# The first and the last microseconds of a two-layer lookup convolution: norm ahead of the sort, transfers in another order, a last image of its own

## The chip, the core and the metric

The kernel runs on one core of one Trainium2 chip, in float32. The metric is the device time of one execution in microseconds, the median of several runs. Six sequences of instructions run side by side: TensorE (PE, with its weight loads PEld), VectorE (DVE), ScalarE (ACT), GpSimd (POOL) and SyncE (SP). Two of them issue transfers here: SP (queue q1 in the profile, "hardware_dynamic") and POOL (queue q0, "software_dynamic"). Both queues share 16 DMA engines.

## The reference

The input x has 16 images of 256 channels and 28 x 28 pixels. With g = the group norm of x (32 groups of 8 channels), the result is x + block(g), where block is two lookup convolutions with batch norms, a squeeze-and-excite gate, and a residual:

```python
def amm_conv3x3(x, centroids, w_sub):
    p = patches3x3(x)                            # (b, n, c, 9): 9 taps of every channel
    d = sum(p*p) - 2 * einsum('bncs,cks->bnck', p, centroids) + sum(centroids**2)
    attn = softmax(-d, axis=-1)                  # over 16 codes per channel
    lut = einsum('cks,cso->cko', centroids, w_sub)
    return einsum('bnck,cko->bno', attn, lut)

def block(g):
    out = relu(bn(amm_conv3x3(g, centroids1, wsub1)))
    out = bn(amm_conv3x3(out, centroids2, wsub2))
    s = sigmoid(relu(mean(out) @ w1 + b1) @ w2 + b2)
    return relu(out * s + g)

result = x + block(gn(x))
```

## The kernel before, in words

**Units.** Layer l of image b is cut into two halves of the pixels (384 and 400, `PXT`), and each half into 8 quads `m` of 32 channels. One quad of one half is a unit of 16 blocks: 16 small matmuls for the logits (`logits`, L591; 32 records in the profile), an exponential on ACT (`b_exp`, L643), 16 small matmuls with the codes (`b_num`, L653), two transposes and a reciprocal on DVE (`b_turn`, L665, L671), a scaling on POOL (`c_scale`, L681 to L693), a transpose on DVE (`c_turn`, L699), and dense matmuls with the weights (`c_look`, L717). After the 8 quads of a half, `evacuate` takes the sums from PSUM on ACT: into the image `ims[1]` for layer 1 (L729), into `y` with a running sum for layer 2 (L739). In layer 2, quad 0 is done with row maxima (`MAXED`), and its logits come five slots early.

**The plan.** `Plan` is a table from (slot, position) to calls; `emit` walks it in order, so it fixes each engine's program by hand. One slot holds one unit; a stage is one layer of one image, 16 slots. Stages run (layer 1 of image 0), (layer 1 of image 1), (layer 2 of image 0), (layer 1 of image 2), and so on, 32 stages or 512 slots. The last position of a slot, REST, holds the side work: loads, norms, shifts, patch writes.

**Patches.** The 9 taps are laid out in DRAM first. `shift` (ACT, L485 and L487) makes two copies of an image, moved by one column (`sides`); `to_pat` (L496) writes the image and the two copies to a DRAM buffer `pat`, 12 pieces in the order `STEPS` (half of the partitions h, column dx, block k); `patches` (L577, SP) reads a unit's rows from there with four transfers, three slots ahead. Units 0 to 3 of a half need the six pieces with h = 0. `prep` issues 12 pieces with all 784 pixels (588 KB), `prep_near` 24 pieces, the 384 pixels of the first half (288 KB) ahead of the 400 of the second (300 KB).

**Start.** SP and POOL load image 0 (`load_x`, POOL, L150) and the constants (SP). DVE and PE sort the channels: keys (`sort_keys`, L272 to L290), ranks (`sort_ranks`, L298 to L308), then the layer-1 weights by matmuls with the permutation (`sort_ws1(0)` to `sort_ws1(5)`, L333). `square_codes` (POOL, L419) and `setup_codes` (L426, L427) finish the codes. Group norm is `gn_stats` (DVE, L444), `gn_mean` and `gn_var` (PE, ACT, POOL), `gn_apply` (ACT, L475). Layer 2's weights are fetched by POOL with indirect transfers (`fetch_ws2`, L406, 18 of them), its codes are placed by SP (`place_wd2`, L365, `place_cw2`, L374).

**End of an image.** `se_hidden` and `se_gate` make the gate, `se_scale` (DVE, L536, L537) finishes it; then, in four blocks of 392 pixels, `gate` (ACT, L547), `finish` (DVE, L553, adds the normed image), `relu` (ACT, L557) with `residual` (POOL, L561) or `relu_residual` (DVE, L565), and one `store` (POOL, L568).

**Fallback.** POOL keeps running totals of the softmax sums. At the end DVE takes their extremes (`good`, L928, L929), PE and DVE count them into a flag (`bad`, L935), every engine loads the flag (L936), and behind it stands `tc.If(flag > 0)` with a loop that does all images again with maxima everywhere (L937). With these inputs the branch goes past it. The program's closing drains and barrier stand under L1031.

Of the kernel before, what the change touches and what calls it, by code (L numbers as in the profile page):

```python
# [72 lines left out]
def kernel(  # L73
# [74 lines left out]
    def load_x(b, xb):  # L148
        t = xpool.tile([P, NB, HW], F32, tag="xt", name="xt")
        nc.gpsimd.dma_start(t, xb.rearrange("(b p) n -> p b n", p=P))  # L150
        xs[b] = t

    load_x(0, x[0])


# [137 lines left out]
    def sort_ranks(row):  # L293
        own = small.tile([P, NB], F32, name="key_own")
        rank = small.tile([P, NB], F32, name="rank")
        for b in range(NB):
            dg = scratch(P)
            nc.vector.tensor_mul(dg, row[:, b * P : (b + 1) * P], ident)  # L298
            nc.vector.tensor_reduce(own[:, b : b + 1], dg, axis=AX.X, op=ALU.add)

            gt = scratch(C)
            eq = scratch(C)
            nc.vector.tensor_scalar(gt, row, own[:, b : b + 1], None, op0=ALU.is_gt)
            nc.vector.tensor_scalar(eq, row, own[:, b : b + 1], None, op0=ALU.is_equal)
            nc.vector.tensor_mul(eq, eq, earlier[:, b])
            nc.vector.tensor_add(gt, gt, eq)
            nc.vector.tensor_reduce(rank[:, b : b + 1], gt, axis=AX.X, op=ALU.add)
            nc.vector.tensor_scalar(perm[:, b], ranks, rank[:, b : b + 1], None, op0=ALU.is_equal)  # L308
# [258 lines left out]
    def store(b, ob):  # L567
        nc.gpsimd.dma_start(ob.rearrange("(b p) n -> p b n", p=P), ys.pop(b)[0])  # L568
        for d in (se, nrm, xs):
            d.pop(b)  # L570

# [178 lines left out]
    class Plan:  # L750
        def __init__(self, step, lead, lb):
            self.step = step
            self.lead = lead
            self.lb = lb
            self.ns = len(PXT) * NQ * step
            self.lc = LC if step == 1 else 3
            self.end = self.ns + self.lc * step
            self.jobs = {}
            self.tiles = []
            self.loads = []  # L760
# [56 lines left out]
        def prep(self, l, pat, t, pace=1):  # L817

            for i, dx in enumerate((0, 2)):
                for k in range(NB):  # L820
                    self.at(t + (2 * i + k if pace == 1 else i), REST, shift, l, dx, k)
            for i in range(len(STEPS)):
                self.at(t + int(i * pace), REST, to_pat, l, i, pat)

        def prep_near(self, l, pat, t):

            for i, dx in enumerate((0, 2)):
                for k in range(NB):
                    self.at(t + i, REST, shift, l, dx, k)
            n = len(STEPS) // 2  # L830
            for i, (dx, k, h) in enumerate(STEPS):
                self.at(t + i // 2, REST, to_pat, l, i, pat, *PXT[0])

                self.at(t + 6 if dx == 1 else t + 7 + 3 * h + (i - n * h - NB) * 3 // 4, REST, to_pat, l, i, pat, *PXT[1])

        def norm(self, b, t):
# [5 lines left out]
            for k in range(NB):  # L842
                self.at(t + k, REST, gn_apply, b, k)

        def close(self, b, ob, te, pace):
# [11 lines left out]
            self.at(te + 5 + 3 // pace, REST, store, b, ob)  # L857
# [11 lines left out]
    bn_setup()  # L869
    row = sort_keys()  # L870
    square_codes()
    for k in range(NB):
        for i in range(2):
            gn_stats(0, k, i)
    gn_mean(0)
    gn_var(0)
    sort_ranks(row)
# [3 lines left out]
    for i, (dx, k, h) in enumerate(STEPS[: len(STEPS) // 2]):  # L881
        if dx != 1:
            shift(0, dx, k)
        to_pat(0, i, d_pat[0], *PXT[0], eng=nc.gpsimd if dx == 0 else nc.sync)
    sort_bn()
# [3 lines left out]
    for si, (l, b) in enumerate(stages):  # L889
        t = si * NS  # L890
        plan.stage(l, b, pat_of(l, b), t, () if l == 0 else MAXED)
        if l == 0 and b >= 1:
            n0 = 7 if b == 1 else t - 2 * NS + 1
            plan.at(n0 - (8 if b == 1 else 11), REST, load_x, b, x[b])
            plan.norm(b, n0)
            plan.prep(0, pat_of(0, b), {1: 9, 2: 33, 3: 57}.get(b, t - 2 * NS + 3), 0.67 if b == 1 else 1)
        if l == 1:
            if b in (0, B - 1):
                plan.prep_near(1, pat_of(1, b), t - NS + LC)
# [3 lines left out]
            plan.close(b, out[b], t + NS + LC, 1 if b < B - 2 else 4)  # L903
    for i in range(len(STEPS) // 2, len(STEPS)):
        plan.at(-1, REST, to_pat, 0, i, d_pat[0], *PXT[0], nc.sync)
    for i in range(len(STEPS)):
        plan.at(i * 5 // len(STEPS), REST, to_pat, 0, i, d_pat[0], *PXT[1])
    for i, (slot, pos) in enumerate(((-1, REST), (-1, REST), (-1, REST), (0, LOOK_A), (1, LOOK_A), (1, LOOK_B))):
        plan.at(slot, pos, sort_ws1, i)
        if i % 2:  # L910
            plan.at(slot, REST, ones_row, pts[3 + i // 2])
# [4 lines left out]
    for g in range(NLT):  # L916
        plan.at(6 + g, REST, fetch_ws2, g)
# [6 lines left out]

    good = small.tile([P, 2], F32, name="good")
    for i, lim in enumerate((S_MAX, 1.0 / S_MIN)):
        t = small.tile([P, 1], F32, name="ext")
        nc.vector.tensor_reduce(t, totals[i], axis=AX.X, op=ALU.max)  # L928
        nc.vector.tensor_scalar(good[:, i : i + 1], t, lim, None, op0=ALU.is_le)  # L929
# [7 lines left out]
    with tc.If(flag > 0):  # L937
        with tc.For_i(0, B) as bi:
            load_x("g", x[bass.ds(bi, 1)].rearrange("o c n -> (o c) n"))
            plan = Plan(8, 3, 5)  # L940
# [7 lines left out]
            plan.at(s1 + plan.end - 4, REST, load_x, "g", x[bass.ds(bi, 1)].rearrange("o c n -> (o c) n"))  # L948
# [86 lines left out]
```

## Time and profile before

| | us |
|---|---|
| median of 3 runs | 2786.48 (2784.22 to 2790.07) |
| the profiled execution, its own time | 2784.22 |
| its span (first to last instruction) | 2782.7 |
| first logits matmul | 39.95 |
| last matmul of the lookups ends | 2759.7 |
| flag ready (L935) | 2769.81 |
| mean granted TensorE clock | 0.991 |

The page gives busy times over the whole span. Most of the span is one pattern of 32 slots, repeated, so the page's shares tell of that pattern; the two ends show only in answers to a window: the timeline, the chain of waits, busy time by stretch, and transfers by queue. A unit's beginning is read from the timeline's L591 rows, one group of 32 records per unit. Times in them count from the span's start.

### The profile page before, as it was taken

To read this page: it belongs to the slowest core of one execution; us is meant where nothing else is said; L and a number is where in the kernel's file an instruction comes from. 1 tells how busy PE (TensorE), PEld (TensorE's weight loads), DVE (VectorE), ACT (ScalarE), POOL (GpSimd) and SP (SyncE) were. 2 spreads that over 40 slices of the span, in tenths; PEclk is the share of its full clock that TensorE was granted. 3 is DMA by queue.
4 is the path that set the end of the run, shared out by engine and by line. 5 is a ranking of instruction groups with operands and counts; after the bars stand their busy time and mean duration, and the time that the engine had idled before them with its cause. 6 is when DMAs were issued, how large, how long until landed. Compare 5 with 4: busy or idle time off the path is not lost.

```text
span 2782.7 us, 90173 instructions
## 1 busy us (share of the span) xinstructions
PE 2706.4 (97%) x37748; PEld 1081.3 (39%) x37748; DVE 2180.1 (78%) x2645; ACT 1093.1 (39%) x1595; POOL 1902.7 (68%) x2714
## 2 busy tenths in 40 slices
PE   6999999999999999999999999999999999999996
PEld 3333333333333343333333333333333334333332
DVE  4667788887878878788887888778787787878885
ACT  2333443434334343443434334343443434334332
POOL 3786676766677677676766677667676766766763
PEclk9999999999999999999999999999999999999998
DMA  7887888767677676777767678676777767674551
GB/s 215 214 215 190 224 218 211 200 174 199 171 206 208 165 200 162 206 196 182 201 174 199 176 201 212 159 199 165 207 197 182 199 172 203 176 191 114 143 139 37
DMA packets 230825, 514.99 MB, mean 185 GB/s; under 512 B 34184, under 2 KB 185608, under 8 KB 230408
## 3 DMA queue, kind: packets, MB, share of 16 engines
q0 software_dynamic: 51824, 269.50, 36.7%
q1 hardware_dynamic: 178584, 239.62, 33.3%
q8 instruction: 299, 4.90, 0.7%
q14 instruction: 118, 0.97, 0.1%
HBM read 264.64 MB, written 244.37 MB: 183 GB/s over the span
## 4 chain that ended last, share of the span: by engine, by line
PE 85%; DVE 8%; issue 3%; POOL 2%; DMA 1%; ACT 0%; SPq 0%; DVEq 0%; POOLq 0%; ACTq 0%
PE acc L717 54%; PE pair L591 15%; PE pair L653 14%; DVE nt L665 3%; DVE q L699 1%; DVE rc L671 1%; DVE e L629 1%; POOL k L681 1%; DMA pat<-side 0%; POOL pat L496 0%; POOL total L693 0%; PE pair L333 0%; DMA pt<-pat 0%; PE pair L524 0%; DVE gn_st L444 0%
## 5 line engine op out<-in xcount | busy, mean ns | idle before, releaser
L717 PE MATMUL acc<-q,ws 128*128 128x384 f32 (+1 forms) x4096 | 1635.2, 518 | 4.5 <-ACT im L729 4.5
L665 DVE STREAM_TRANSPOSE nt<-pair 128x832 f32<-128x832 f32 (+1 forms) x1024 | 978.3, 993 | 528.2 <-PE pair L653 441.0
L681 POOL TENSOR_TENSOR k<-nt,rc 128x832 f32<-128x832 f32 (+1 forms) x512 | 803.8, 1570 | 825.8 <-DVE rc L671 786.9
L643 ACT ACTIVATE e<-pair 128x768 f32<-128x768 f32 (+1 forms) x960 | 740.2, 821 | 1045.2 <-PE pair L591 1044.5
L717 PEld LDWEIGHTS acc<-q,ws 128*128 128x128 f32 x4096 | 699.9, 189 | 889.6 <-issue 555.2
L591 PE MATMUL pair<-pt,wd 19*32 19x384 f32 (+1 forms) x16384 | 519.4, 501 | 27.4 <-DVE nt L665 17.2
L699 DVE STREAM_TRANSPOSE q<-k 128x832 f32<-128x832 f32 (+1 forms) x512 | 488.7, 954 | 0.8 <-POOL k L681 0.8
L653 PE MATMUL pair<-e,cw 32*32 32x384 f32 (+1 forms) x16384 | 484.6, 501 | 0.3 <-DVE nt L665 0.2
L671 DVE RECIPROCAL rc<-nt 128x104 f32<-128x104 f32 (+1 forms) x512 | 398.7, 779 | 17.6
L591 PEld LDWEIGHTS pair<-pt,wd 19*32 19x32 f32 x16384 | 125.5, 103 | 341.0 <-issue 241.7
L687 POOL TENSOR_TENSOR tail<-nt,rc 128x104 f32<-128x104 f32 (+1 forms) x512 | 243.1, 475 | 0.0
L653 PEld LDWEIGHTS pair<-e,cw 32*32 32x32 f32 x16384 | 119.8, 103 | 288.4 <-issue 169.9
L717 PE MATMUL acc<-qt,ws 128*128 128x400 f32 (+1 forms) x512 | 215.2, 502 | 0.0
L693 POOL TENSOR_TENSOR total<-total,nt 128x96 f32<-128x96 f32 (+1 forms) x480 | 213.3, 444 | 0.0
L693 POOL TENSOR_TENSOR total<-total,rc 128x96 f32<-128x96 f32 (+1 forms) x480 | 188.1, 392 | 0.0
L496 POOL DMA_DIRECT2D pat<-side x274 | 185.4, 677 | 3.4 <-ACT side L485 3.0
L636 ACT ACTIVATE e<-e 128x768 f32<-128x768 f32 (+1 forms) x64 | 54.9, 857 | 191.1 <-DVE e L629 190.0
L717 PEld LDWEIGHTS acc<-qt,ws 128*128 128x128 f32 x512 | 93.4, 190 | 88.6 <-issue 30.2
L729 ACT ACTIVATE im<-acc,bnsh,bnsc 128x384 f32<-128x384 f32 (+1 forms) x64 | 43.4, 679 | 149.6 <-PE acc L717 139.4
L621 POOL TENSOR_TENSOR z<-z,mx 128x768 f32<-128x768 f32 (+1 forms) x64 | 99.0, 1546 | 0.0
L496 POOL DMA_DIRECT2D pat<-im x136 | 92.4, 680 | 0.0
L739 ACT ACTIVATE y<-acc,bnsh,bnsc 128x384 f32<-128x384 f32 (+1 forms) x64 | 43.5, 679 | 89.4 <-PE acc L717 85.0
(121 smaller groups left out, 901.4 us busy)
## 6 DMA issues: line engine op xcount, KB each, us to landing
pat<-side POOLq DMA_DIRECT2D x232, 588.0 KB, 5.7
pt<-pat SPq DMA_DIRECT2D x1024, 112.5 KB
pt<-pat SPq DMA_DIRECT2D x1024, 108.0 KB
pat<-im POOLq DMA_DIRECT2D x116, 588.0 KB, 5.3
xt<-in_x POOLq DMA_DIRECT2D x32, 784.0 KB, 7.2
out_dram<-y POOLq DMA_DIRECT2D x16, 784.0 KB, 6.4
pat<-side POOLq DMA_DIRECT2D x24, 300.0 KB, 6.5
pat<-side POOLq DMA_DIRECT2D x18, 288.0 KB, 3.3
```

The source lines that it names most:

```text
L496: eng.dma_start(view(pat, (ROWS * p0 + 9 * k + 3 * dx) * HW + px, [[ROWS * HW, m], [HW, 3], [1, n]]), bass.AP(v.tensor, v.offset, [list(v. ...
L591: nc.tensor.matmul(ps[t // 2][c : c + 32, t % 2, :n], lhsT=wd[l][32 * i : 32 * i + rows, 4 * u["m"] + t, :], rhs=u["pt"][32 * i : 32 * i + ...
L621: nc.gpsimd.tensor_tensor(z, z, mx.unsqueeze(2).to_broadcast(list(z.shape)), ALU.subtract)
L643: nc.scalar.activation(e[:, :, :n], ps[:, :, :n], AF.Exp, scale=2.0)
L653: nc.tensor.matmul(u["nm"][t // 2][32 * i : 32 * i + 32, t % 2, :n], lhsT=cw[l][c : c + 32, 4 * u["m"] + t, :], rhs=es[t // 2][c : c + 32, ...
L665: nc.vector.transpose(nt[:, :nb, 2 * v : 2 * v + 2].rearrange("p b t r -> p t b r"), ps[:, :, : 32 * nb].rearrange("p t (b r) -> p t b r", ...
L671: nc.vector.reciprocal(rc[:, : 8 * nb], u["nt"][:, :, SUM])
L681: nc.gpsimd.tensor_tensor(q[:, :nb].rearrange("p b (a s) -> p (b a) s", s=8), nt[:, :, :8], rc.unsqueeze(2).to_broadcast([P, 8 * nb, 8]), ...
L687: nc.gpsimd.tensor_tensor(tails[key][:, :nb, 8 * (m % 4) : 8 * (m % 4) + 8], nt[:, :, 8].rearrange("p (b a) -> p b a", a=8), rc.rearrange( ...
L693: nc.gpsimd.tensor_add(t[:, : 8 * nb], t[:, : 8 * nb], v)
L699: nc.vector.transpose(q[:, :, : 32 * nb].rearrange("p h (b r) -> p h b r", r=32), u.pop("k")[:, :nb].rearrange("p b (h r) -> p h b r", h=2),)
L717: nc.tensor.matmul(accs[key][:, :n], lhsT=ws[l][:, 2 * m + h if h < 2 else 2 * NQ + m // 4, o * P : (o + 1) * P], rhs=u["q"][h][:, :n], st ...
```

## The change

It edits the order at the start, the writes and loads of the first three images, the end of the last image, and which queue the fallback uses. The body's units stay as they are.

- `load_x(0)` goes to SP, ahead of the constants. The statistics, mean and variance of image 0 stand ahead of the sort; on POOL `square_codes` follows the norm. In `sort_ranks` two fused operations stand for four.
- Image 0, first half: the six pieces with h = 1 go from SP (slot -1, behind the first patch reads) to POOL (slot -2, behind its two pieces with h = 0), and the load of image 1 follows them on POOL. The second half's pieces are spread over slots 1 to 5. One `sort_ws1` stands ahead of `sort_bn`, and the later ones one place earlier.
- Image 1: `prep_near` (24 pieces over slots 9 to 20) in place of `prep` (12 pieces over slots 9 to 16). The load of image 2 goes from slot 6 to 11, its norm five slots later; the 18 fetches go out three in four slots, from slot 8. The layer-2 pieces of image 0 start one slot later, those of its second half stay.
- Last image: `close_last` replaces `gate` and `finish` by one DVE operation per block that uses the normed image still held in `ims[0]` (`gate_norm`); two blocks go on with `relu` and `residual`, two with `relu_residual`; SP stores each half of the channels by itself. The totals' extremes are taken before the gate (`watch`).
- In the fallback all transfers that POOL issued go to SP.

```diff
-    load_x(0, x[0])
+    load_x(0, x[0], nc.sync)
...
-            nc.vector.tensor_scalar(gt, row, own[:, b : b + 1], None, op0=ALU.is_gt)
-            nc.vector.tensor_scalar(eq, row, own[:, b : b + 1], None, op0=ALU.is_equal)
-            nc.vector.tensor_mul(eq, eq, earlier[:, b])
-            nc.vector.tensor_add(gt, gt, eq)
+            nc.vector.scalar_tensor_tensor(eq, row, own[:, b : b + 1], earlier[:, b], op0=ALU.is_equal, op1=ALU.mult)
+            nc.vector.scalar_tensor_tensor(gt, row, own[:, b : b + 1], eq, op0=ALU.is_gt, op1=ALU.add)
...
+    def gate_norm(b, k, i):
+        y, gt = ys[b][0][half(k, i)], se[b]
+        im = ims[0][:, k, W + i * (HW // 2) : W + (i + 1) * (HW // 2)]
+        nc.vector.scalar_tensor_tensor(y, y, gt[:, k : k + 1], im, op0=ALU.mult, op1=ALU.add)
+
+    def store_block(b, ob, k):
+        nc.sync.dma_start(ob[k * P : (k + 1) * P], ys[b][0][:, k])
...
+        def close_last(self, b, ob, te):
+            self.at(te, SMALL, se_hidden, b)
+            self.at(te + 1, SMALL, se_gate, b)
+            at = lambda *a: self.at(te + 1, REST, *a)
+            at(se_scale, b)
+            for i in range(2):
+                at(gate_norm, b, 0, i)
+                at(relu, b, 0, i)
+                at(residual, b, 0, i)
+            for i in range(2):
+                at(gate_norm, b, 1, i)
+                at(relu_residual, b, 1, i)
+            for k in range(NB):
+                at(store_block, b, ob, k)
...
+    def watch():
+        for i, lim in enumerate((S_MAX, 1.0 / S_MIN)):
+            t = small.tile([P, 1], F32, name="ext")
+            nc.vector.tensor_reduce(t, totals[i], axis=AX.X, op=ALU.max)
+            nc.vector.tensor_scalar(good[:, i : i + 1], t, lim, None, op0=ALU.is_le)
...
-    bn_setup()
-    row = sort_keys()
-    square_codes()
     for k in range(NB):
         for i in range(2):
             gn_stats(0, k, i)
+    bn_setup()
     gn_mean(0)
     gn_var(0)
+    row = sort_keys()
+    square_codes()
     sort_ranks(row)
...
-            n0 = 7 if b == 1 else t - 2 * NS + 1
+            n0 = {1: 7, 2: 22}.get(b, t - 2 * NS + 1)
...
-            plan.prep(0, pat_of(0, b), {1: 9, 2: 33, 3: 57}.get(b, t - 2 * NS + 3), 0.67 if b == 1 else 1)
+            if b == 1:
+                plan.prep_near(0, pat_of(0, b), 9)
+            else:
+                plan.prep(0, pat_of(0, b), {2: 33, 3: 57}.get(b, t - 2 * NS + 3))
...
-                plan.prep_near(1, pat_of(1, b), t - NS + LC)
+                plan.prep_near(1, pat_of(1, b), t - NS + LC + (1 if b == 0 else 0), t - 6)
...
     for i in range(len(STEPS) // 2, len(STEPS)):
-        plan.at(-1, REST, to_pat, 0, i, d_pat[0], *PXT[0], nc.sync)
+        plan.at(-2, REST, to_pat, 0, i, d_pat[0], *PXT[0])
     for i in range(len(STEPS)):
-        plan.at(i * 5 // len(STEPS), REST, to_pat, 0, i, d_pat[0], *PXT[1])
+        plan.at(1 + i // 3 if i < 6 else i // 2, REST, to_pat, 0, i, d_pat[0], *PXT[1])
...
-        plan.at(6 + g, REST, fetch_ws2, g)
+        plan.at(8 + g * 4 // 3, REST, fetch_ws2, g)
...
-            plan = Plan(8, 3, 5)
+            plan = Plan(8, 3, 5, nc.sync)
```

## The prediction

> **What bounds the kernel now.** I read the page first, then the windows by stretch, the chain of waits of the first 130 us, the DMA view of one crowded stretch, and the end. The page gives the frame:
>
> ```profile
> span 2782.7 us, 90173 instructions
> PE 2706.4 (97%) x37748; PEld 1081.3 (39%) x37748; DVE 2180.1 (78%) x2645; ACT 1093.1 (39%) x1595; POOL 1902.7 (68%) x2714
> ```
>
> PE sets the pace. By the starts of the L591 groups in the timeline (one group is one unit), 32 units take 167.34 us, and from unit 64 to 448 no such stretch is over 0.4 us longer. This body issues the same instructions in both kernels, so I expect nothing of it. What can be won lies before unit 24 and behind the last matmul. The windows (us, PE busy, PEld, DVE, ACT, POOL, PE clock, DMA share, GB/s) show a good stretch, one with stalls, and the end:
>
> ```profile
> 78.38:113.92 35.54, 35.54 (x513) 14.23 (x512) 26.81 (x34) 17.19 (x23) 32.45 (x51) 1.00 0.75 186
> 113.92:174.81 60.89, 58.04 (x734) 21.74 (x733) 38.30 (x47) 21.81 (x30) 46.10 (x68) 0.97 0.83 202
> 2760.00:2784.00 24.00, 0.99 (x8) 0.71 (x8) 6.29 (x14) 4.60 (x11) 3.04 (x3) 0.60 0.10 38
> ```
>
> The first is units 6 to 12 (seven, 5.08 us each), the second units 13 to 22 (ten, 6.09 each). Ten at 5.08 are 50.8, so 10 us are lost there, though PE looks busy. The chain (start, us, what) names the early losses:
>
> ```profile
> 24.35 12.59 DMA pat<-side
> 37.08 0.31 SPq L577
> ...
> 39.27 0.56 DMA pt<-pat
> 39.95 4.26 PE pair L591 x32
> ...
> 114.37 8.32 DMA pt<-pat
> 122.74 1.44 PE pair L591 x26
> ```
>
> The first logits wait for the patch writes of image 0, units 14 on for patch reads. Both are transfers pushed aside by others, as the DMA view of 25 to 28 us shows (packets, MB, share of 16 engines):
>
> ```profile
> q0 software_dynamic: 119, 0.47, 76.0%
> q1 hardware_dynamic: 82, 0.12, 19.6%
> ```
>
> With both queues full, POOL's queue moves 0.157 MB/us and SP's 0.041.
>
> **Start: -5.5 us (0 to -7.5).** *Norm.* The statistics start at 11.95, behind the sort keys; the page's median of 7.2 us from issue to landing puts xt (issued 1.59) at 8.8. Moved to the head of SP's queue (issue 1.02, 0.8 MB at about 0.39 MB/us), I put its landing at 5, between 4 and 8.8. The statistics now stand behind gmat's scaling and a read of vecs, which queues behind xt: start 6.5 (5.5 to 9). From the start of the statistics to gn_apply were 19.46 - 11.95 = 7.5 us, so gn_apply starts at 14.0, 5.5 earlier. Every other load of SP's queue moves back by one issue (0.45 us); none was waited for that closely. The three squares (POOL, 2.2 us) now follow the norm, until 16.2, ahead of POOL's first write, which waits for side until 16.6 anyway. On PE sort_keys now queues behind gn_var, and DVE begins the keys 2.4 us later, behind the statistics; four operations of the ranks fewer give back 1.3. Both are hidden: the ranks end near 19.5 (20.2 before), and with sort_bn and three sort_ws1 (9.7 us) PE is ready near 30.5, ahead of the patches; without that cover it would be up to 2 us.
>
> *Writes.* The loads keep the DMA full until about 16.5, so the writes start there, not at 21.9. Units 0 to 3 need six pieces of 0.295 MB: four on SP, two on POOL. POOL's first bytes came 2.4 us after its first issue (22.46, nothing to speak of before 24.8), so SP's first two pieces flow alone from 16.5 to 19.2 at 0.2 MB/us, 0.54 MB. Then 0.64 MB remain on SP beside a full POOL queue, for directly behind its two first-half pieces the change puts all six second-half ones and only then the load of image 1. At 0.041 to 0.055 MB/us that is 12 to 16 us, done at 31 to 35; I take 31.5 against 37.08: -5.5. The end at 0 is the case in which POOL's eight pieces hold SP's back as long as the load and three wider pieces did before.
>
> The Trainium skill (DMA: Bandwidth & Descriptors, section Queues, rings and completion order) says that an engine goes round robin between queues, a whole packet from each. It speaks against filling POOL's queue here; with packets of equal size it would give SP half of 0.2 MB/us, 6.4 us instead of 12 to 16 and writes done near 26, where the row above gives a fifth.
>
> *Units 0 to 6.* The 36 matmuls of sort_ws1 in units 0 and 1 stay 36, with 12 of them moved ahead of unit 1's logits; the six writes between SP's third and fourth patch tile (43.35 to 50.28) are gone. But units 3 to 5 wait for POOL and for find_rows (2.1 us at L396), which stay: 0 (to -2, inside the range).
>
> **Image 1: -5 us (-1 to -8).** Before, 12 pieces of 588 KB go out in units 9 to 16 with a fetch of 128 KB in each: 0.96 + 0.13 MB per 5.1 us unit is 0.21 MB/us, over the 0.157, so SP's reads fall to 0.041 to 0.05 where a unit's 0.44 MB needs 0.086, and after three units of read-ahead PE waits. After, the same bytes are 24 pieces over units 9 to 20, with three fetches in four units: 0.69 to 0.71 MB per unit, 0.137 MB/us. The body lives with 0.6 MB per unit in 12 of 16 units without a stall. So the bulk of the 10 us goes, and I keep 5 for what stays: 0.137 is close to 0.157, and the load of image 2 falls into unit 11. POOL issues 12 more DMAs (0.68 us each, 8 us over 12 units): with 2.9 us of c_scale, 1.4 for two writes and 1.2 for a fetch it has 5.4 us in three units of four and 4.3 in the fourth, under PE's 5.1 to 5.3 on average; if that cover goes, up to 3 us, in the bound. Late next is the side tile: shift for layer 2 at units 21 and 22 overwrites what the writes of units 19 and 20 read; they landed in 6.5 us (page), the room is 10. ACT's wait at 207 (10.1 us, 4.5 of them PE's) comes from writes of unit 26 that don't move, and stays. The norm of image 2, five units later, has ten units of room: 0.
>
> **End: -7 us (-3.5 to -8).** The timeline's end (start, us), and the sequencers' own instructions of L937 and L1031 behind it (duration min/median/max in ns, first and last start):
>
> ```profile
> 2765.82 2.67 DVE L565 SCALAR_TENSOR_TENSOR y<-y,xt 128x392 f32<-128x392 f32 x2
> 2769.04 0.73 POOL L568 DMA_DIRECT2D out_dram<-y  x1 [0.98 <-POOL y L561]
> 2769.67 0.14 DVE L935 TENSOR_SCALAR bad<-count 1x1 int32<-1x1 f32 x1
> ```
>
> ```profile
> L937 POOLq INC_SWDGE_SEM  x1: 1396/1396/1396, 2775.5 to 2775.5; - x1
> ...
> L1031 POOLq DRAIN  x3: 46/103/4972, 2776.9 to 2782.5; - x3
> ```
>
> The flag is ready at 2769.81; then load, branch and the jump past the fallback (PE's branch 5.5 us), POOL's semaphore step, POOL's drain of 4.97, and 0.8 of barrier. *To the flag:* from 2762.65, gate and finish (3.25 us) become six DVE operations. At 0.61 alone and 1.31 beside POOL's two residuals (2763.9 to 2766.2) they end at 2767.5; the good/ext operations (0.8 us) move to DVE's idle 7.2 us before L536. Flag near 2767.9: -1.9. SP issues both stores before it reads the flag (0.4 us behind it); they land during the jump. The skill (SBUF — State Buffer, section Who interferes with whom) has a DVE operation with two SBUF inputs and a reading POOL operation block each other wholly; taken so, four operations and two residuals of 1.0 in series end at 2768.3, 0.8 later than by the rows. *Behind the flag:* POOL loses its store and, with no POOL DMA left in the fallback, the semaphore step (1.4). The long drain follows that step directly; the other two take 0.05 and 0.10. I take it to shrink to that: then PE's jump and SP's thirteen waits end the run near 2774.9 + 0.8, 7 us earlier. If the drain stays at 4.97, the end gains 3.5.
>
> **Sum.** -5.5 - 5 - 7 = -17.5. The profiled execution took 2784.2 (span 2782.7 and 1.5 around it), 2.3 below the median of 2786.5. So 2766.7 in its terms, **2769** in the median's.
>
> **Rivals.**
> - *POOL's drain stays* (it is the queue's own, not the step's): for it, nothing here shows a drain without that step at the end; against it, the two short ones. -14: 2772.5. Chance 0.14.
> - *The first patches are no earlier*, since the change doesn't leave them alone: six POOL pieces replace one load and three pieces. For it, the 0.157 to 0.041; against, the head start of 5 us. -12: 2774.5. Chance 0.12.
> - *Image 1's stalls return in other units* (the bytes are the same): -12.5: 2774. Chance 0.06.
> - *Slower: starved patch reads over units 9 to 20.* If POOL's queue never empties, a unit's reads take 0.44/0.041 = 10.7 us, 5.6 over its pace. Twelve units less three of read-ahead are +50, less the 10 lost today, less 12.5 from start and end: +28, 2814. It beats the gains from eight starved units on, and decides once POOL's bytes pass 0.157 x 5.1 = 0.80 MB per unit; 0.71 are planned, unit 11 has 1.4. Chance 0.05.
>
> **Numbers.** The forecast has 0.60; 0.03 are left for all terms at their near ends (-4.5). The range goes from all far ends together (-23.5, 2763) over the first three rivals to 2778 (-8.5, two terms failing by half); outside are the rest of the near ends and the slow case. 0.2% (5.6 us) is what a measurement of this kernel can tell: faster 0.92 (the forecast and the first three rivals), same 0.03, slower 0.05.
>
> **What would show it.** gn_apply at 14, SP's first patch read at 31 to 32, the first logits near 34 instead of 39.95; units 13 to 22 within 56 us; at the end no INC_SWDGE_SEM, POOL's drains under 0.2, and the flag 8 us ahead of the end instead of 13. Wrong if L577 stays at 36 or later, if ACT waits at L485/L487 in units 21 and 22, or if the stretch from unit 64 on changes its 167.34.

## The result and the profile after

The changed kernel took 2775.06 us (median of 4 runs, 2772.23 to 2776.79) against 2786.59 us: a ratio of 0.9957, 95% interval [0.9939, 0.9974], faster by 11.5 us. The forecast was 2769 us with a range of 2763 to 2778. The profiled execution took 2772.23 us. The head of its page (compare the span, 2782.7 before, and PE's and POOL's busy time):

```profile
span 2770.4 us, 90183 instructions
PE 2700.0 (97%) x37748; PEld 1080.9 (39%) x37748; DVE 2178.4 (79%) x2641; ACT 1091.2 (39%) x1591; POOL 1912.0 (69%) x2730
```

PE executes the same 37748 matmuls. Where the 12.3 us of the two spans lie is read from the starts of the logits groups (L591 before, L598 after; one group is one unit) and from the end:

| stretch | before, us | after, us | change | predicted |
|---|---|---|---|---|
| to the start of unit 8 | 88.62 | 87.91 | -0.7 | -5.5 |
| units 8 to 23 | 91.52 | 83.91 | -7.6 | -5 |
| units 24 to 31 | 43.17 | 44.86 | +1.7 | 0 |
| units 32 to 499 | 2452.97 | 2452.42 | -0.5 | 0 |
| units 500 to 510 | 64.65 | 63.19 | -1.5 | 0 |
| unit 511 to the flag (bad) | 28.88 | 26.78 | -2.1 | -1.9 |
| flag to the end | 12.9 | 11.4 | -1.5 | -5.1 |

Each column is one execution. The experiments below show how far such numbers repeat where their edits don't reach. The start is the changed kernel's in seven of them (e3 to e8, e10): with the changed kernel's own trace, the first logits stand at 37.5 to 39.0 and unit 8 at 86.1 to 90.7, so the -0.7 can't be told from 0. Units 13 to 22 take 51.7 to 53.2 us in five (e5 to e8, e10), and from unit 511 to the end it is 37.2 to 38.2 us in five (e1 to e4, e9). So the -7.6 and the -3.6 of the last two rows together stand clear of this scatter.

So one term came, larger than predicted (image 1), the first half of the end came as predicted, and two terms hardly came (the start, and what lies behind the flag). The lines below show these places.

**Start.** The chain of waits (start, us, what) of the changed kernel:

```profile
13.42 1.98 ACT im L473 x2
...
18.30 8.73 DMA pat<-side
...
27.16 11.14 DMA pt<-pat
...
38.44 3.87 PE pair L598 x32
42.31 6.50 PE pair L331 x24
...
67.50 2.13 issue
69.63 1.07 PE pair L394 x8
70.70 0.86 PE pair L598 x32
71.56 3.83 PE acc L724 x6
```

gn_apply starts at 13.42, a little before the predicted 14.0. SP reads the first patches at 27.16, ten us earlier than before and four earlier than predicted. But from there to the first logits it now takes 11.3 us, 11.14 of them in the read, where the kernel before took 2.9 (37.08 to 39.95), and the logits start at 38.44 instead of 39.95. The DMA view of 26 to 32 us says why (packets, MB, share of 16 engines):

```profile
q0 software_dynamic: 359, 1.39, 99.6%
...
q1 hardware_dynamic: 2, 0.00, 0.1%
```

In these 6 us POOL's queue (q0) moves 359 packets and SP's (q1) moves two. POOL has put the six pieces with h = 1 and the load of image 1 ahead of the reads. The rest of the chain shows the gain going back: at 71.56 six matmuls take 3.83 us. In the chain of the kernel before, the same six took 2.13:

```profile
73.97 2.13 PE acc L717 x6
```

The window of that place in the changed kernel has the clock (third column from the end, the granted share) at one half:

```profile
71.82:75.23 3.41, 3.41 (x6) 1.35 (x4) 0.00 (x0) 1.30 (x2) 0.04 (x1) 0.50 0.64 233
```

**Image 1 and the units behind it.** The windows by stretch, in the columns of the prediction's table (units 8 to 23, 13 to 22, 24 to 31):

```profile
87.91:171.82 83.91, 83.08 (x1171) 32.98 (x1171) 61.23 (x75) 37.61 (x50) 74.67 (x112) 1.00 0.80 213
113.51:166.49 52.98, 52.15 (x734) 20.54 (x733) 39.84 (x51) 19.79 (x28) 49.70 (x76) 1.00 0.86 239
171.82:216.68 44.86, 38.68 (x543) 14.72 (x542) 29.65 (x35) 12.19 (x16) 35.94 (x51) 0.92 0.79 207
```

Units 13 to 22 take 52.98 us where they took 60.89, under the 56 that the prediction named. In units 24 to 31 PE's work is the same 38.7 us as before, and the idle time has grown. The kernel before had there:

```profile
180.14:223.31 43.17, 38.64 (x543) 14.72 (x542) 29.43 (x35) 12.19 (x16) 31.70 (x47) 0.92 0.80 225
```

The chain of the changed kernel there:

```profile
188.02 1.03 POOL ws L404
...
189.07 1.65 POOL k L688
...
193.17 6.92 DMA pat<-im
...
200.11 0.04 ACTq L736
```

A weight fetch (L404) now stands in POOL's list ahead of the pieces whose landing (6.92 us, 6.45 before) ACT waits for at unit 28.

**End.** The last operations (start, us), then the sequencers' own instructions of the branch (L976) and of the end (L1070; duration min/median/max in ns, first and last start):

```profile
2758.27 0.57 DVE L563 SCALAR_TENSOR_TENSOR y<-y,xt 128x392 f32<-128x392 f32 x1
...
2758.93 0.14 DVE L974 TENSOR_SCALAR bad<-count 1x1 int32<-1x1 f32 x1
```

```profile
L976 PEldq COMPARE_BRANCH  x1: 4315/4315/4315, 2759.8 to 2759.8; - x1
```

```profile
L1070 POOLq DRAIN  x3: 46/103/6034, 2763.6 to 2770.2; - x3
```

The flag (bad) is ready at 2759.07. The semaphore step (INC_SWDGE_SEM) is gone, as predicted. The drain behind it, predicted to shrink from 4.97 us to 0.1, is 6.03 us. So the 1.5 us behind the flag are made of three changes: the semaphore step and the waits ahead of it are gone (about -1.7), the drain is longer (+1.1), and the jump is shorter (POOL is past it 3.7 us after its branch instead of 4.7, and PE's branch takes 4.3 us instead of 5.5). The prediction has no term for the last, and why it is shorter is not shown.

### The profile page after: what moved, and what is told of

It is laid out like the page before. It is cut to its first block, busy times and chain, and to the rows that moved or that the text cites. A ratio compares the mean times of both kernels' runs of the same rounds, so it can differ in the third digit from the quotient of the medians.

```text
span 2770.4 us, 90183 instructions
## 1 busy us (share of the span) xinstructions
PE 2700.0 (97%) x37748; PEld 1080.9 (39%) x37748; DVE 2178.4 (79%) x2641; ACT 1091.2 (39%) x1591; POOL 1912.0 (69%) x2730
## 4 chain that ended last, share of the span: by engine, by line
PE 86%; DVE 8%; issue 3%; POOL 1%; DMA 1%; ACT 0%; DVEq 0%; SPq 0%; ACTq 0%; POOLq 0%
PE acc L724 55%; PE pair L598 16%; PE pair L660 15%; DVE nt L672 3%; DVE q L706 1%; DVE rc L678 1%; DVE e L636 1%; DMA pt<-pat 0%; POOL k L688 0%; PE pair L331 0%; DMA pat<-side 0%; POOL pat L494 0%; PE pair L522 0%; DVE gn_st L442 0%; DMA pat<-im 0%
## 5 line engine op out<-in xcount | busy, mean ns | idle before, releaser
L724 PE MATMUL acc<-q,ws 128*128 128x384 f32 (+1 forms) x4096 | 1634.8, 518 | 6.2 <-ACT im L736 6.2
L724 PEld LDWEIGHTS acc<-q,ws 128*128 128x128 f32 x4096 | 699.8, 189 | 890.5 <-issue 554.5
L598 PE MATMUL pair<-pt,wd 19*32 19x384 f32 (+1 forms) x16384 | 513.5, 501 | 23.5 <-DVE nt L672 16.1
L598 PEld LDWEIGHTS pair<-pt,wd 19*32 19x32 f32 x16384 | 124.7, 103 | 332.5 <-issue 240.6
L724 PE MATMUL acc<-qt,ws 128*128 128x400 f32 (+1 forms) x512 | 215.2, 502 | 0.0
L494 POOL DMA_DIRECT2D pat<-side x286 | 193.1, 676 | 2.6 <-issue 1.4
L724 PEld LDWEIGHTS acc<-qt,ws 128*128 128x128 f32 x512 | 93.4, 190 | 88.6 <-issue 30.2
```

What stands on the lines that cost most here:

```text
L494: eng.dma_start(view(pat, (ROWS * p0 + 9 * k + 3 * dx) * HW + px, [[ROWS * HW, m], [HW, 3], [1, n]]), bass.AP(v.tensor, v.offset, [list(v. ...
L598: nc.tensor.matmul(ps[t // 2][c : c + 32, t % 2, :n], lhsT=wd[l][32 * i : 32 * i + rows, 4 * u["m"] + t, :], rhs=u["pt"][32 * i : 32 * i + ...
L724: nc.tensor.matmul(accs[key][:, :n], lhsT=ws[l][:, 2 * m + h if h < 2 else 2 * NQ + m // 4, o * P : (o + 1) * P], rhs=u["q"][h][:, :n], st ...
```

## The experiments

All are built on the changed kernel, so each is compared with its 2775.06 us and its landmarks; ratios are to the kernel before. By their times alone e1, e2, e3 and e10 can't be told from the changed kernel, for the intervals overlap; e1's median is 4.7 us lower, and yet the profiled executions of the two have spans within 0.1 us of each other. So these readings rest on landmarks, each of one trace.

**e1_load_first: the load of image 1 moved.**

```
  load_codes = lambda: nc.sync.dma_start(cw[1], cw2)
+ load_x(1, x[1], nc.sync)
...
- plan.at(n0 - (8 if b == 1 else 11), REST, load_x, b, x[b])
+ if b > 1:
+     plan.at(n0 - 11, REST, load_x, b, x[b])
```

> The changed kernel with one edit: the load of image 1 (0.8 MB) is issued from SP behind the constants, ahead of the first patch writes, and no longer from POOL behind eight pieces. Theory (POOL's queue shuts out SP's patch reads while it holds anything): the six second-half pieces still keep POOL's queue full until about 32, the load no longer until 37. The first logits, 38.44 in the changed kernel, come at 35 to 36, 2.5 to 3.5 earlier; the patch writes start 2 us later and stay hidden. Rival (the first patch read's 11.1 us are its own, not the queue's): the first logits stay within 0.5 of 38.4, or move 2 later with the writes.

Measured: 2770.40 us, ratio 0.9944 [0.9927, 0.9961]. The first logits stand at 35.26, in the theory's 35 to 36: 0.8 MB less in POOL's queue brings them 3.2 us forward although SP issues the reads later, at 31.75 instead of 27.16: from the issue to the logits it is 3.5 us in place of 11.3. But unit 4 is only 1.5 us earlier and unit 8, at 87.81, 0.1 (half clock at unit 5 lasts 6.83 us here, 3.41 in the changed kernel). So the shut-out explains the first logits, and it does not explain where their gain goes.

**e2_halves_on_sp: the six pieces with h = 1 moved.**

```
- plan.at(-2, REST, to_pat, 0, i, d_pat[0], *PXT[0])
+ plan.at(-1, REST, to_pat, 0, i, d_pat[0], *PXT[0], nc.sync)
```

> The changed kernel with one edit: the six second-half pieces of image 0 go out on SP behind the first three patch tiles, no longer on POOL ahead of them; the load of image 1 stays on POOL. Theory (shut-out by POOL's queue): only the load (0.8 MB) is left there, issued at 18 to 20 and through by about 27, so the reads issued at 27.2 flow at once and the first logits stand at 31 to 32, where PE has the sorted weights ready (30.99 in the changed kernel). Unit 8, 87.91 in the changed kernel, at 81 to 84. Rival (the reads are slow by themselves): first logits within 1 us of 38.4. Second rival (the pieces on SP hold back patch tiles 3 and 4 as in the kernel before): first logits at 31 to 32, but unit 8 back at 87 to 89.

Measured: 2768.51 us, 0.9937 [0.9919, 0.9954]. First logits at 32.32, 6.1 us earlier (the theory said 31 to 32; the pieces that the reads wait for land at 29.24, where they landed at 27.03 in the changed kernel). Unit 8 stands at 85.02: 2.9 us are left, between the theory's 81 to 84 and the second rival's 87 to 89, and what took them is neither: unit 3 is still 4.4 us ahead. The chain names it:

```profile
30.10 4.04 DMA pt<-pat
...
34.18 2.30 PE pair L598 x28
36.48 7.97 PE pair L331 x24
44.46 0.89 PE pair L598 x32
...
63.16 2.13 issue
65.28 1.56 PE pair L394 x8
66.85 1.51 PE pair L598 x32
68.36 4.14 PE acc L724 x6
```

The 24 sorting matmuls (L331) between the logits of units 0 and 1 take 7.97 us, 6.50 in the changed kernel: PE had idled ahead of unit 0 and ran at half clock from 34.87 to 41.69. Behind the 2.13 us that PE waits for DVE's part of the row search, the eight matmuls of L394, the logits and the six of L724 again run at half clock (65.59 to 72.41). So each slow stretch comes with a pause of PE's ahead of it; that the pause is what causes it is argued here, not shown.

**e3_fetch_dense: the fetches as before.**

```
- plan.at(8 + g * 4 // 3, REST, fetch_ws2, g)
+ plan.at(6 + g, REST, fetch_ws2, g)
```

> The changed kernel with one edit: the 18 weight fetches go one per unit from unit 6 on, as in the kernel before, instead of three in four units from unit 8 to 30. Theory (POOL's bytes against 0.157 MB/us): 0.59 MB of pieces and 0.13 MB of fetch per 5.1 us are 0.140 MB/us, still under it, so units 13 to 22 stay at 52 to 54 us (52.98 in the changed kernel); and with no fetch in unit 25 ahead of the writes that ACT waits for, units 24 to 31 go from 44.86 back to 43.2, 1.6 less. Rival (spreading the fetches is what freed image 1): units 13 to 22 at 57 or more.

Measured: 2775.73 us, 0.9965 [0.9954, 0.9975]. Units 13 to 22 took 58.53 us: the rival's side, and the theory of bytes fails here. The chain of these units is POOL, one unit after the other; one of them, and what follows the last:

```profile
138.91 1.64 POOL k L688
140.54 0.41 POOL tail L694
140.96 0.77 POOL total L700 x2
141.72 1.26 POOL pat L494 x2
142.98 0.30 issue
143.28 1.02 POOL ws L404
...
158.61 7.55 DMA pat<-side
```

The products, two pieces and a fetch are 5.4 us of POOL's own work per unit, over PE's 5.1 to 5.3. POOL falls behind unit by unit until layer 2's shift waits for the landing of the late pieces (7.55 us). The second half of the expectation holds: with no fetch behind unit 23, units 24 to 31 take 43.37 us instead of 44.86.

**e4_whole_pieces: image 1 in whole pieces.**

```
- plan.prep_near(0, pat_of(0, b), 9)
+ for i in range(len(STEPS)):
+     plan.at(9 + int(i * 0.67), REST, to_pat, 0, i, pat_of(0, b))
```

(The shifts stay in units 9 and 10.)

> The changed kernel with one edit: the patch writes of image 1 go out as 12 whole pieces of 588 KB over units 9 to 16, as in the kernel before, with the fetches still spread. Theory (POOL's bytes): 0.88 MB of pieces and 0.10 MB of fetch per 5.1 us are 0.19 MB/us, over 0.157, so the stalls come back: units 13 to 22 at 58 to 61 us instead of 52.98, the run 6 to 8 us longer. Rival (the spread fetches alone freed image 1): units 13 to 22 stay at 52 to 54.

Measured: 2782.96 us, 0.9984 [0.9974, 0.9993]. Units 13 to 22 took 61.39 us: the theory. The chain has one starved read of 7.57 us, and PE's half clock behind it:

```profile
131.08 7.57 DMA pt<-pat
...
138.70 2.15 PE pair L598 x28
140.85 2.97 PE acc L724 x4
```

So image 1's gain of 7.9 us in units 13 to 22 needs both edits: with whole pieces SP's reads are starved, with dense fetches POOL is late. Either alone leaves 58 to 61 us.

**e5_no_fallback to e8_last_load_on_sp: the end, each by one edit.** Their diffs, in this order:

```
- flag = nc.values_load(bad[0:1, 0:1])
- with tc.If(flag > 0):
-     with tc.For_i(0, B) as bi:
...
```

```
  with tc.If(flag > 0):
-     with tc.For_i(0, B) as bi:
...
+     nc.vector.memset(good, 0.0)
```

```
- load_x("g", x[bass.ds(bi, 1)].rearrange("o c n -> (o c) n"), nc.sync)
- plan = Plan(8, 3, 5, nc.sync)
+ load_x("g", x[bass.ds(bi, 1)].rearrange("o c n -> (o c) n"))
+ plan = Plan(8, 3, 5)
...
```

```
- plan.at(t + NS, REST, load_x, b, x[b])
+ plan.at(t + NS, REST, load_x, b, x[b], nc.sync if b == B - 1 else nc.gpsimd)
```

> The changed kernel without the fallback: the flag is neither read nor branched on, and the branch's body (never entered with these data) is gone. Theory J (POOL's long drain belongs to the jump over the fallback, its code being fetched again): POOL's last drains all under 0.2 us, the end about 1 us behind the landing of the last store, some 8 us earlier than in the changed kernel. Rival Q (the drain is the queue's own and stays whatever precedes): a drain of 5 to 6 us, begun when POOL's last residual is done, so the end only 5 to 6 us earlier.

> The changed kernel with the branch kept and its body cut to one small memset (never entered with these data). Theory J: what is jumped over is already there, so branch and drain together take under 2 us instead of 9.8. Rival Q: the jump shortens (PE's branch 4.3 us to under 1), POOL's drain stays at 5 to 6.

> The changed kernel with the fallback's loads, patch writes and stores issued from POOL again, as in the kernel before. The prediction's step (the semaphore step costs 1.4 and the long drain hangs on it): INC_SWDGE_SEM of 1.4 us comes back, and the drain stays as it is, 6.0, so the end is 1.4 later. Rival (the drain ends at a time of its own, and the step only fills part of it): INC_SWDGE_SEM 1.4, drain about 5.0, the end within 0.5 us.

> The changed kernel with one edit: the last load of the last image (the residual's input, POOL's last transfer, 14 us before the flag) is issued from SP. Theory J: POOL's drain stays at 6.0, the end moves by less than 0.5 us. Rival (the drain winds up POOL's last transfers): the drain under 2 us.

One run each: 2765.70, 2768.58, 2773.40 and 2772.27 us; 2787.36 for the kernel before beside them. POOL's drains, in this order for e5, e6 and e7 (with e7's semaphore step):

```profile
L1055 POOLq DRAIN  x3: 46/97/8148, 2755.1 to 2763.7; - x3
```

```profile
L1058 POOLq DRAIN  x3: 46/103/6034, 2760.0 to 2766.6; - x3
```

```profile
L976 POOLq INC_SWDGE_SEM  x1: 1652/1652/1652, 2763.3 to 2763.3; - x1
```

```profile
L1070 POOLq DRAIN  x3: 46/103/6034, 2765.0 to 2771.6; - x3
```

With the branch gone the drain is still there (e5: its sequencer reaches it at 2755.07, POOL's last residual ends at 2757.16, the drain at 2763.22, 6.06 later). With almost nothing to jump over it is 6.034 (e6), behind the semaphore step 6.034 (e7), with POOL's last transfer taken away 5.952 (e8). So neither the jump nor the semaphore step nor POOL's last transfer makes the drain (rival Q in e5 and e6; in e7 and e8 it stays, as expected). It ends some 6 us after POOL reaches it or, in e5, after the end of POOL's last residual. POOL issues transfers in every run, so whether the drain belongs to the engine or to its transfer queue is not separated. e6 shows what the jump costs by itself: from unit 511 to the end 34.6 us instead of 38.1. e7 shows the semaphore step (1.65 us, 1.4 expected), with the five waits ahead of it: 40.2 us, 2.1 longer.

**e9_start_cleared: the start's causes together.** e1 and e2, and the row search split, its DVE part (find_by) one unit ahead of its PE part:

```
- plan.at(4, REST, find_rows)
+ plan.at(4, REST, find_by)
+ plan.at(5, REST, find_rows)
```

> The changed kernel with three edits in the start: the load of image 1 behind the constants on SP (as in the first experiment), the six second-half pieces on SP behind three patch tiles (as in the second), and the row search's DVE part (4 small products) one unit ahead of its PE part, so that PE does not wait for it. Theory (POOL's queue shuts out the reads; then PE's idle stretches drop its clock to a half for whole windows of 3.4 us, which gave the gain of the second experiment back): first logits at 31 to 32, directly behind the sorted weights, unit 1 at 39 to 41 (48.73 in the changed kernel, 44.39 in the second experiment), no 2.1 us wait between units 4 and 5, unit 8 at 76 to 80 (87.91 and 85.02). Rival (the start is held by PE's own sorting work, whatever the reads do): unit 1 at 44 or later, unit 8 at 84 to 85.

Measured: 2762.54 us, 0.9918 [0.9902, 0.9935]. First logits 31.08, unit 1 at 38.93, unit 8 at 77.62, all within the theory's numbers or 0.1 of them; unit 32 at 206.88 against 216.68. The chain:

```profile
28.11 4.45 DMA pt<-pat
...
32.61 0.92 PE pair L605 x26
33.53 5.47 PE pair L332 x24
39.00 0.86 PE pair L605 x32
```

The 24 sorting matmuls take 5.47 us at full clock, and PE goes from its first sorting work to the logits with hardly a pause. That the missing pause is what keeps the clock up is not shown: e12 below has the same start up to here, but PE pauses for 0.89 us ahead of its first logits (30.41), the clock is at half from 32.38 to 39.21, and unit 1 stands at 42.26.

**e10_end_and_unit28: the end's cause, and the wait at unit 28.**

```
     def watch():
...
+        ps = bank()
+        nc.tensor.matmul(ps[0:1, 0:2], lhsT=ones_sq[:, 0:1], rhs=good, start=True, stop=True)
+        count = small.tile([1, 1], F32, name="count")
+        nc.vector.tensor_reduce(count, ps[0:1, 0:2], axis=AX.X, op=ALU.add)
+        nc.vector.tensor_scalar(bad, count, -1.0, 2.0 * P, op0=ALU.mult, op1=ALU.add)
...
-    at(relu, b, 0, i)
-    at(residual, b, 0, i)
+    at(relu_residual, b, 0, i)
...
+    if first and dx == 1:
+        self.at(s - 1, REST, to_pat, l, i, pat, *PXT[1], nc.sync)
...
-    plan.at(8 + g * 4 // 3, REST, fetch_ws2, g)
+    plan.at(8 + g * 4 // 3 if g < 13 else (28, 29, 30, 31, 31)[g - 13], REST, fetch_ws2, g)
```

(first holds for layer 2 of image 0 alone.)

> The changed kernel with edits at two places far apart, each read from its own stretch. Units 24 to 31: no fetch in units 25 to 27, and the four pieces that ACT's write of layer 2's input waits for go out on SP a unit earlier. Theory (that wait is 6.7 us of PE idle and 2 more of half clock): 44.86 becomes 36.5 to 39. Rival (SP's reads, now behind four pieces, run late): 41 to 45. End: the flag is worked out ahead of the last gating, and both blocks' residuals are on DVE, so POOL has nothing left to do and reads the flag 10 us earlier. Theory (POOL's drain is 6.03 of its own and starts when POOL reaches the end of its list): drain and jump of POOL lie beside the gating, the end is DVE's jump behind the last residual; from unit 511 to the end 31 to 33 us instead of 38.2. Rival (a drain cannot run beside the other engines' work, or DVE's eight operations are slower than DVE and POOL together): 37 to 39.

Measured: 2765.90 us, 0.9931 [0.9915, 0.9948]. The end is 32.3 us from unit 511 (38.1): the drain is as long as ever, but stands beside the gating:

```profile
L1073 POOLq DRAIN  x3: 46/103/5952, 2754.2 to 2763.6; - x3
```

It begins at 2754.2 and is over at 2760.1, while DVE's last residual ends at 2757.8 and DVE and SP still have their jumps to make. DVE's eight operations take 0.62 and 0.57 us each with POOL silent, where two of them took 1.26 and 1.37 beside POOL's residuals. Units 24 to 31, at 43.35, follow the rival: the four pieces were issued at 189 to 190 behind SP's own reads and landed at 198.2.

**e11_all_places and e12_fetch_late: one kernel from all of it.** e11 joins e9 and e10, with the four pieces on SP at units 21 to 24 and the gathered code tables in a still unused part of the weight tile; e12 puts the pieces back on POOL and the last eight fetches at units 28 to 35. The lines that neither e9 nor e10 has, of e11 and then of e12:

```
+ self.at(t + 2 * h + k, REST, to_pat, l, i, pat, *PXT[1], nc.sync)
...
- t = scratch(NB * m).rearrange("p (b m) -> p b m", b=NB)
+ t = ws[1][:, 14 if m0 == 0 else 16 :].rearrange("p g c -> p (g c)")[:, : NB * m].rearrange("p (b m) -> p b m", b=NB)
```

```
- self.at(t + 2 * h + k, REST, to_pat, l, i, pat, *PXT[1], nc.sync)
...
+ plan.at(8 + g * 4 // 3 if g < 10 else 18 + g, REST, fetch_ws2, g)
```

> The changed kernel with everything that the runs before point to: the start of the ninth run, the end of the tenth, no fetch in units 25 to 27, and two edits more: the four pieces that ACT's write waits for at unit 28 go out on SP one per unit from unit 21 on (in the tenth run they were issued at 189, behind SP's reads, and landed at 198.2), and the two sorted code tables are gathered in a part of the weight tile that is not filled until unit 28, so that POOL's product does not wait 6.6 us for their stores as in the ninth run. Theory: first logits at 31, unit 8 at 74 to 77 (77.62 in the ninth run), units 24 to 31 in 36.5 to 40 us (43.35 in the tenth), from unit 511 to the end 32.3, the run at 2748 to 2756. Rival (the waits only change their name: reads starved by what was moved to SP): units 24 to 31 at 42 or more, or units 8 to 24 longer than the 84.2 of the ninth run, the run at 2757 or more.

> The eleventh kernel with the four pieces back on POOL at unit 26, as in the changed kernel, and the last eight weight fetches behind unit 27, one per unit at 28 to 35 (four of them were POOL's work in units 21 to 25 of the changed kernel, 1.3 us each). Theory (in units 21 to 26 POOL's list of products, pieces and fetches is the late one, so that taking fetches out brings the pieces, and ACT's write that waits for their landing, forward by up to 5.3 us; SP's reads are left alone): units 24 to 31 in 38 to 41 us (44.86 in the changed kernel, 47.37 in the eleventh run), the run at 2746 to 2750. Rival (the pieces are late by their 6 to 8 us of landing, not by POOL's list): 43 to 45, the run at 2751 to 2754.

Measured: e11 2755.22 us, 0.9887 [0.9870, 0.9903]; e12 2753.86 us, 0.9886 [0.9870, 0.9903]. Both beat both kernels, by 32 to 33 us on the kernel before and 20 to 21 on the changed one; between themselves they can't be told apart. e11's time lies in the theory's 2748 to 2756, e12's in the rival's 2751 to 2754. At e11's start the theory holds (unit 8 at 75.73), at units 24 to 31 the rival: 47.37 us, longer than ever. ACT's wait is gone and a starved read has its place:

```profile
183.11 5.49 DMA pt<-pat
...
188.64 1.63 PE pair L605 x26
190.27 2.96 PE acc L731 x4
```

e12 leaves SP's reads alone and takes 43.77 there, the rival's 43 to 45: PE, not POOL's list, is on the chain until 173.2, in unit 26; then come POOL's product and its four pieces, and the landing (5.95 us) is still waited for. No arrangement tried went under the 43.17 of the kernel before; whether one can is open.

## Why the prediction was right, and where it was not

The measured 2775 us lies in the range of 2763 to 2778, but the sum of 17.5 us missed by 6, and that it missed by no more is in part luck. The start and the end fell short by 8.1 us together. Units 8 to 23 gave 2.6 us more than was put for them, and 1.5 came from units 500 to 510, whose clock was not in the sum.

**Start, -5.5 predicted, -0.7 measured.** The norm's step was right (14.0 against 13.42), and the writes were through four us earlier than the step put them: from 18.30 to 27.03 SP moved 0.75 MB beside POOL's 1.37, 0.086 MB/us, where the step had 0.041 to 0.055. The estimate that the prediction set beside it, a half share and writes done near 26, came closer. Two steps failed.

The first is the tacit one behind "first logits near 34": that the reads take about 2.5 us once the writes are done. The prediction had priced what POOL's full queue does to SP's writes (0.041 to 0.055 MB/us), and had the same six pieces and the load standing there; it did not ask what they do to the reads that follow. They got 2 packets in 6 us. The rival "the first patches are no earlier" was thus right in what it would cost (the whole of this term), and wrong in place: the writes were earlier, the reads were not. e1 and e2 showed it, by 3.2 and 6.1 us of first logits.

The second is that a gain at the first logits was carried through to unit 8. It would not have been: e2 has the 6.1 us and keeps 2.9. The prediction counted 36 sorting matmuls before and after and put the cost of moving 12 of them at 0; it named PE's wait for the row search and rightly left it as it was (2.1 us), but did not ask for the clock behind such a wait. e9 takes the load, the pieces and the wait for the row search out together and is 10.3 us ahead at unit 8; the part of each is not separated.

**Image 1, -5 predicted, -7.9 in units 13 to 22.** The mechanism and its place were right: starved reads (e4). The size was cut to half for what might stay, and little stayed: 52.98 against the 50.8 of unhindered units. The side remark on POOL's list (5.4 us in three units of four, hidden on average) was the better half of the working: e3, which has that fetch in every unit, loses 5.5 us to it. The expectation of e3 had gone by bytes alone, and was wrong. In the working, the 0.96 MB of pieces per unit before the change are 0.90 (twelve of 0.60 MB over eight units); with the fetch that is 0.20 MB/us, still over 0.157.

**Units 24 to 31, 0 predicted, +1.7.** The failed step is "comes from writes of unit 26 that don't move". Their unit did not move, but the fetches that were spread reached unit 25, 1.03 us of POOL's list directly ahead. Without the fetches behind unit 23 the stretch takes 43.37 (e3), as before.

**End, -7 predicted, -3.6.** To the flag the sum was right (-1.9 against -2.1), with DVE's operations beside POOL's residuals at 1.26 and 1.37 us, the rows' price of 1.31: two of DVE's six operations took twice their 0.6 us, the others not. The Trainium skill's whole blocking (SBUF — State Buffer, section Who interferes with whom) would, by the prediction's estimate, have had the flag 0.8 later. Behind the flag the step "the long drain follows that step directly, I take it to shrink" failed, and the rival with 0.14 was the case. That its 3.5 us for the whole end are so near the measured 3.6 is partly luck: the drain grew by 1.1 us and the jump shrank by 1.0, and neither was in it. The argument was that two other drains in the same list are short; they are, but they stand behind a first one that has already taken its 6 us. e5 to e8 show the 6 us without the jump, with a short one, behind the semaphore step and without the last transfer. What stays open is why its length differs, from 4.97 in the kernel before over 5.14 (e11) and 5.46 (e9, e12) to 6.12 (e3).

**Not in the prediction: the clock.** Between units 500 and 510 the changed kernel gains 1.5 us with the same instructions: half clock from 2700.08 to 2703.50, where the kernel before had it from 2706.95 to 2713.77, behind the same wait for DVE. In e5 and e10, which leave these units alone, they take 64.7 us, as in the kernel before. At unit 5 it is the other way round: the same wait of 2.1 us cost nothing before and 1.7 after. There, too, the edits are not the reason, for e5 has the changed kernel's start and shows no loss behind the wait:

```profile
67.69 2.13 issue
...
71.74 2.13 PE acc L724 x6
```

In e4, with the same start, the loss is 3.2 us. The whole time follows: of the 17 runs of the kernel before beside e1 to e4, those with a granted clock of 0.992 took 2781.75 to 2787.09 us, those with 0.989 took 2788.46 to 2792.57. In the traces every stretch of half clock is 3.41 us long or two or three times that, but for the last, which the program's end cuts off. The Trainium skill (TensorE: Matmul & The Clock Gate, section Part 1: The HAM clock gate) says that the clock falls to a half after an idle window of about 3.4 us, that the windows run freely, and that the point of the change depends on where in a window the first matmul lands. The durations agree; but a wholly idle window was not needed, for in the 3.41 us ahead of 71.82 PE has 2.19 us of matmuls. So 0 to 3.2 us at unit 5 and 1.5 between units 500 and 510 differ from one execution to the next and are not design, and a prediction of 0.4% has to carry them in its range. That the place in the window decides is the skill's account; no run here sets it.

## What to carry to other kernels

When a change brings a transfer's producer forward, follow the transfer that consumes it too: it goes through the same queues, and a queue filled ahead of it takes back what the earlier write gave. A transfer that can wait costs POOL 0.6 to 0.7 us to issue here, and it kept the reads behind it (11.3 us from their issue to the first logits in the changed kernel, 3.5 in e1); put it behind the first reads, or ahead of everything while nothing else is ready. A drain like POOL's at the end of a program belongs beside the other engines' last work, which won 5.8 us here (e10): give that engine nothing to do in the last microseconds.

## What the runs showed of the hardware

- With POOL's queue full (writes of patches and a load), SP's reads of patches moved 2 packets in 6 us beside POOL's 359. The Trainium skill (DMA: Bandwidth & Descriptors, section Queues, rings and completion order) has the engines take turns between queues by packet, which would give the reads every other packet; this trace does not agree for these reads. For SP's writes just ahead of them it speaks less against it: 536 packets beside POOL's 362 (18.30 to 27.03). Why the reads fare otherwise is not shown here.
- POOL's final drain takes 5.0 to 6.1 us from where POOL reaches it (in e5 from the end of the work still running), with or without a branch, a semaphore step or a late transfer, and can lie beside the other engines' work (e10).
- The jump past the fallback took 3.6 us on DVE, 3.7 on POOL and 4.3 on PE in the changed kernel, 4.7, 4.7 and 5.5 in the kernel before; with a body of one instruction 0.2 on PE (e6).
- PE's pause of 2.1 us at unit 5 cost between 0 and 3.2 us more in matmuls at half clock (0 in the kernel before and in e5, 1.7 in the changed kernel, 3.2 in e4).
